# A Mamba block, cross attention and a gated dense layer on one core: the last chunk's dt, the scan's first loads and the first output projection arranged anew

## The chip, the cores and the metric

The kernel runs on one core of a Trainium2 chip. A core has five engines that run side by side, each working through its own instructions in order: TensorE (PE in the profile; PEld is its weight load), VectorE (DVE), ScalarE (ACT), GpSimd (POOL) and SyncE (SP), which here only issues transfers. ScalarE can issue transfers too; they go to a queue of their own (q10 in the profile, SyncE's is q1). The metric is the time of one execution on the device in microseconds (us), lower is better. The kernel before takes 3256.49 us, the median of three runs (3252.81 to 3258.94).

## The reference, cut to what matters

Four sequences of 1024 tokens with 512 features, all float32. The change touches only the first layer:

```python
h   = x + mamba(rmsnorm(x))            # this part
x   = layernorm(x + h + mlp(rmsnorm(h)))
x   = layernorm(x + cross_attention(x, ctx))
x   = layernorm(x + gated_lora_dense(x))

def mamba(x):                          # 1024 channels d, 16 states n
    u, z = split(x @ in_proj_w.T)
    u    = silu(causal_conv4(u))
    dt_r, B, C = split(u @ x_proj_w.T, [32, 48])
    dt   = softplus(dt_r @ dt_proj_w.T + dt_proj_b)
    h_l  = exp(dt_l * A) * h_(l-1) + dt_l * B_l * u_l      # scan over the tokens l
    y    = sum_n h * C + u * D
    return (y * silu(z)) @ out_proj_w.T
```

## The kernel before, in words

**Chunks.** The 4096 tokens are eight chunks (`NC`) of 512 (`T`). Every chunk goes through `mamba_in` first; then `scan_mlp` scans all chunks while TensorE does the output projection and the MLP of earlier chunks beside it; attention and the dense layer follow.

**`mamba_in`** works in *slots*, eight for each chunk (one for each block of 128 channels). Work that depends on earlier work is entered with `at(d, phase, f)`, for d slots later and one of four phases of a slot. `conv(j)` and `gate(j)` multiply by the input weights on TensorE; ScalarE and VectorE finish u and z; `x_proj` gathers u into one PSUM bank (`ps_xp`, pool `qp`); `project` copies it to `pr` and `bc` on ScalarE; `turn_c` transposes C and `put_c` stores it. For each block j, `dt(j)` is a matmul into one of two PSUM banks (pool `pd`), `dt_softplus` (ScalarE) makes r = dt from it, and for every second block `dt_u` stores r to memory, makes q = dt u on GpSimd (128x1024) and stores that. `put` stores through SyncE's queue. The table `AP` gives the distances: the dt matmuls are two to a slot from the second to the fifth slot after the last `x_proj`, the softplus a slot later, `dt_u` two slots after the matmul. For the last chunk these fall after the last input projection: slots (NC, 0) to (NC, 8) are run inside `mamba_in`, what is left after that (slot 9) in `rest()`, a generator that `scan_mlp` gets as `before`.

**`scan_mlp`** works in *quarters*, four for each step. A step k is one state n of one half chunk (four blocks of 128 channels, `GJ = 4`), 16 steps for a half chunk, 256 in all. In a quarter, VectorE scans one block (`scan`, `hs<-da,hs`), ScalarE makes the next factor (`exp`, `da`, two PSUM banks), GpSimd makes dt u B for half a step ahead in quarters 0 and 1 (`times_b`, `hs<-pk,b`), TensorE transposes the scanned blocks of the step before (`turn`, `ps_h`), and VectorE, or ScalarE with GpSimd, adds them times C to the sum `acc` (`times_c`). At the end of a half chunk `end` enters, some quarters later, the transposes back (`ps_y`), `add_u` (VectorE) and `times_z` (GpSimd), which leaves the finished y of a block; a transfer on ScalarE's queue stores it to memory. For the first two half chunks ScalarE's products wait in the large pool `b_z` (`hz`), which is closed before the MLP's pools (`b_w`, `b_x`, `b_g`: weights, x, hidden) take its room.

**The stream beside it.** From quarter 161 on (`until(GJ * 2 * NS + 33)`) the generator `stream` runs in each quarter after the transposes, paced by an estimate of TensorE's time. For each chunk: `Mlp(c)` loads x (`h`), `load_o` loads the four tiles of the output weights (`wo`, 512 KB each), `load_y` loads the stored y (`wy`, four tiles of 512 KB), `out_proj` multiplies (`ps_o`, 32 matmuls, two at most in a quarter), then a norm (`norm_h`, `norm_sq`, `norm_r`, `norm_x`), transposes (`turns`), and the MLP's products. `norm_r` is the reciprocal root on GpSimd: a scale and `rsqrt_p`, together 14 instructions on 128x4. For chunks 1 to 6, `run` starts the next chunk's projection at quarter 21 after the chunk's last scan. The last chunk is done after the scan.

**What sets the order.** Each engine's instructions are kept in the order of the program text within `mamba_in`, and within `scan_mlp` (`InOrder`), except SyncE's. Between the two functions, and on SyncE, the order is the compiler's, which places an instruction where its own time line says that it is ready. A new tile waits for the last use of the memory that it takes over.

Of the kernel before, what the change touches and what calls it, by code (L numbers as in the profile page):

```python
# [19 lines left out]
P = 128  # L20
# [4 lines left out]
NS = 16  # L25
# [124 lines left out]
EARLY_STEPS = 4  # L150
# [203 lines left out]
def mamba_in(tc, cn, a, dr, sx):  # L354
# [9 lines left out]
    with ExitStack() as ctx:  # L364
        up = sx.enter_context(open_pool(tc, "a_u", bufs=8, side="right"))
        pd = sx.enter_context(open_pool(tc, "a_pd", bufs=2, space=PSUM, side="right"))
        wp = ctx.enter_context(open_pool(tc, "a_w", bufs=1))
# [4 lines left out]
        qp = ctx.enter_context(open_pool(tc, "a_q", bufs=1, space=PSUM))  # L372
# [63 lines left out]
        class Step:  # L436
# [82 lines left out]
            def x_proj(self, j):  # L519
                if j == 0:  # L520
                    self.xp = qp.tile([P, T], F32, tag="xp", name="ps_xp")
                nc.tensor.matmul(
                    self.xp, wxp[:, j], self.u[j // 2][:, j % 2], start=j == 0, stop=j == KI - 1
                )
                if j == KI - 1:
                    at(1, 0, self.project)
                    at(1, 0, self.project_rest)
                    for b in range(KI):
                        at(*AP["b"][b], self.dt, b)
# [24 lines left out]
            def turn_c(self):  # L554

                ps = pp.tile([P, NT, P], F32, tag="mm", name="ps_c")
# [4 lines left out]
            def put_c(self, ps):  # L561
                ct = self.bc[:, 0 : NT * NS].rearrange("p (t n) -> p t n", n=NS)
# [8 lines left out]
            def dt(self, j):  # L571
# [6 lines left out]
                at(*AP["ds"], self.dt_softplus, j, ps, self.dts[jp][:, i])  # L578
                if i:
                    at(*AP["du"], self.dt_u, jp)  # L580
# [4 lines left out]
            def dt_u(self, jp):  # L585
# [3 lines left out]
                nc.gpsimd.tensor_tensor(q, r, self.u.pop(jp), ALU.mult)  # L589
# [55 lines left out]
        for n in range(9):  # L645
            slot(NC, n)

    def rest():
        n = 9
# [8 lines left out]
def scan_mlp(tc, cn, a, dr, before, bx, then):  # L658
# [8 lines left out]
    with ExitStack() as ctx, ExitStack() as sx:  # L667
# [11 lines left out]
        zps, tw = [], []  # L679

        class Step:
# [10 lines left out]
            def load(self, jp, q):  # L692

                pk = pks[self.g, jp, q] = kp.tile([P, 2, T], F32, tag=f"pk{q}", name=f"pk{q}")
                nc.sync.dma_start(pk, dr["pk"][self.c][2 * self.half + jp][:, :, q])
# [6 lines left out]
            def load_b(self):  # L702
                bs[self.k] = bp.tile([P, 1, T], F32, tag="b", name="b")
                nc.sync.dma_start(
# [128 lines left out]
            def times_z(self, i, y):  # L833
                nc.gpsimd.tensor_tensor(y[1], y[1], uzs.pop((self.g, i))[:, 1], ALU.mult)
                jp, jj = divmod(GJ * self.half + i, 2)
                at(1, 3, nc.scalar.dma_start, dr["y"][self.c][jp][:, jj], y[1])
# [11 lines left out]
        class Mlp:  # L848


            def __init__(self, c):
                self.c = c
                self.h = xp.tile([P, NT, D], F32, tag="h", name="h", bufs=2)
                nc.sync.dma_start(self.h, tokens(a["x"], c))
                self.ws, self.ps, self.gs, self.w3s = {}, {}, {}, []

            def w3_tile(self, name, late):
# [3 lines left out]
                return wp.tile([P, 2, D], F32R, tag="w3", name=name, bufs=4)  # L861

# [8 lines left out]
            def load_y(self):  # L871
                for jp in range(KI // 2):
# [10 lines left out]
            def out_proj(self):  # L883
# [7 lines left out]
                ys, ws = self.ys, self.wo  # L891
                for t in range(NT):
                    ps = pp.tile([P, D], F32, tag="mm", name="ps_o")
                    for j in range(KI):
                        jp, jj = divmod(j, 2)
                        nc.tensor.matmul(
                            ps, ys[jp][:, jj, t * P : (t + 1) * P], ws[jp][:, jj],
# [241 lines left out]
        for jp in range(2):  # L1139
            for i in range(2):  # L1140
                step(0).load(jp, i)
        step(0).load_c()
        for k in range(2):
            step(k).load_b()
        for jp in range(2):
            step(0).times_b(jp)
        for i in range(2):
            step(0).exp(i)
        for k in range(EARLY_STEPS):
            for q in range(GJ):  # L1150
                quarter(k, q, lambda: q % 2 or next(before, None))
        assert next(before, 0) == 0
        bx.close()
        with ExitStack() as zx:
# [4 lines left out]
            for k in range(EARLY_STEPS, 2 * NS + 8):  # L1159
# [31 lines left out]
        def first(mlp):  # L1191
            mlp.load_o()
# [10 lines left out]
        def last():  # L1203
            mlp = Mlp(NC - 1)
            yield from first(mlp)
# [4 lines left out]
        for k in range(2 * NS + 8, n + 2):  # L1210
# [855 lines left out]
```

## Time and profile before

| | us |
|---|---|
| median of three runs | 3256.49 |
| lowest, highest | 3252.81, 3258.94 |
| the profiled execution | 3250.26 |
| its span | 3248.5 |

| stretch of the span (us) | what runs there |
|---|---|
| 0 to 488 | `mamba_in` |
| 488 to 508 | dt of the last chunk, first loads of the scan |
| 508 to 2385 | the scan; from 741 on with output projections and the MLP |
| 2385 to 2700 | the last MLP work |
| 2700 to 3248 | attention and the dense layer |

Over the span TensorE is busy 92% of the time, VectorE 83%, GpSimd 73%, ScalarE 61%. The page's second part divides the span into 40 slices of 81 us and gives the busy tenths of each engine; the timeline gives instructions in order of time, several alike merged into one row (x4), with the idle time ahead of a row and what ended it in square brackets. The tiles' names tell the functions apart: nearly all instructions are issued through one helper and so have its line, L308.

### The profile page before, as it was taken

How to read it: one execution, taken by the hardware profiler on the slowest of the kernel's cores; microseconds unless marked ns; L12 is line 12 of the kernel's file. 1: busy time of each engine (PE TensorE's matmuls, PEld its weight loads, DVE VectorE, ACT ScalarE, POOL GpSimd, SP SyncE). 2: the span in 40 equal slices, each digit the busy share in tenths (PEclk: the TensorE clock that was granted, in tenths of full speed). 3: DMA queues.
4: the chain of work that ended last, by engine and by line, in shares of the span. 5: the costliest groups of instructions: out<-in, count | busy, mean ns of one | idle time of the engine just before them, and what ended most of it. 6: DMA issues, size and time to landing. Idle time of an engine off the chain costs nothing.

```text
span 3248.5 us, 47327 instructions
## 1 busy us (share of the span) xinstructions
PE 3001.8 (92%) x15992; PEld 2393.6 (74%) x15992; DVE 2698.2 (83%) x3836; ACT 1973.4 (61%) x3876; POOL 2369.2 (73%) x2169
## 2 busy tenths in 40 slices
PE   7999996887999999999999999999999997999987
PEld 5777773664876786786776786786785887898876
DVE  6876767997999999999999999999962346888876
ACT  3666666776666567666667666667642336666643
POOL 1334328998998999999999999999952115666664
PEclk9999995778999999999999999999999999999998
DMA  4778744336675775675765765765766432111110
GB/s 165 261 264 288 256 167 163 111 104 215 198 224 179 221 223 179 220 226 178 221 223 175 225 217 177 225 213 172 219 190 228 142 104 95 46 46 47 48 41 33
DMA packets 478472, 562.79 MB, mean 173 GB/s; under 512 B 46006, under 2 KB 309814, under 8 KB 477974
## 3 DMA queue, kind: packets, MB, share of 16 engines
q1 hardware_dynamic: 464406, 526.21, 50.6%
q10 hardware_dynamic: 13824, 33.56, 3.2%
q8 instruction: 127, 2.08, 0.3%
q14 instruction: 115, 0.94, 0.1%
HBM read 430.18 MB, written 129.50 MB: 172 GB/s over the span
## 4 chain that ended last, share of the span: by engine, by line
PE 34%; DVE 23%; POOL 12%; issue 8%; DMA 4%; ACT 3%; SPq 0%; ACTq 0%; DVEq 0%; POOLq 0%
DVE hs L308 10%; PE ps_ab L308 10%; POOL hs L308 6%; DVE acc L308 5%; PE ps_m L308 5%; PE ps_h L308 5%; PE ps_o L308 3%; PE ps_s L308 3%; PE ps_b L308 2%; POOL acc L308 2%; PE ps_y L308 2%; DVE g L308 1%; ACT da L308 1%; DMA uz<-pk 1%; DMA w<-w 1%
## 5 line engine op out<-in xcount | busy, mean ns | idle before, releaser
L308 DVE TENSOR_TENSOR_SCAN hs<-da,hs 128x512 f32<-128x512 f32 x1024 | 1214.7, 1207 | 42.7 <-ACT da L308 21.3
L308 POOL TENSOR_TENSOR hs<-pk,b 128x1024 f32<-128x1024 f32 x512 | 1217.2, 2393 | 29.7 <-issue 10.5
L308 ACT ACTIVATE da<-pk,aneg 128x512 f32<-128x512 f32 x1024 | 704.9, 689 | 554.3 <-DVE hs L308 548.6
L308 PE MATMUL ps_ab<-xn,w 128*128 128x512 f32 x3072 | 827.6, 406 | 0.0
L308 PE MATMUL ps_h<-ident,hs 128*128 128x128 f32 x4096 | 684.8, 292 | 91.0 <-DVE hs L308 47.3
L308 PEld LDWEIGHTS ps_h<-ident,hs 128*128 128x128 f32 x4096 | 535.5, 149 | 313.9 <-DVE hs L308 80.5
L308 PEld LDWEIGHTS ps_ab<-xn,w 128*128 128x128 f32 x3072 | 545.0, 189 | 95.8 <-issue 1.1
L308 PE MATMUL ps_m<-w,gs 128*128 128x512 f32 x1536 | 419.3, 408 | 9.5 <-POOL gs L308 9.5
L308 DVE SCALAR_TENSOR_TENSOR acc<-ps_h,c,acc 128x512 f32<-128x512 f32 x542 | 394.2, 727 | 37.8 <-PE ps_h L308 35.6
L308 POOL TENSOR_TENSOR acc<-acc,hc 128x512 f32<-128x512 f32 x232 | 300.1, 1293 | 52.9 <-ACT hc L308 51.5
L308 PEld LDWEIGHTS ps_m<-w,gs 128*128 128x128 f32 x1536 | 274.4, 191 | 61.7 <-POOL gs L308 14.5
L308 PE MATMUL ps_o<-wo,wy 128*128 128x512 f32 x512 | 247.8, 602 | 8.4 <-DMA wy<-y 5.1
L308 ACT ACTIVATE hc<-ps_h,c 128x512 f32<-128x512 f32 x344 | 231.3, 673 | 12.6 <-PE ps_h L308 12.5
L308 POOL TENSOR_TENSOR gs<-g,gs 128x512 fp32r<-128x512 f32 x128 | 165.8, 1295 | 85.1 <-ACT gs L308 85.1
L308 PE MATMUL ps_in<-xn,wu 128*128 128x512 f32 x768 | 214.7, 428 | 0.1
L308 POOL TENSOR_TENSOR pt<-pw,pt 128x512 fp32r<-128x512 f32 x48 | 62.7, 1306 | 194.9 <-ACT pt L308 131.2
L308 PE MATMUL ps_in<-xn,wz 128*128 128x512 f32 x768 | 191.8, 397 | 1.0 <-POOL wz L308 0.6
L308 PEld LDWEIGHTS ps_in<-xn,wu 128*128 128x128 f32 x768 | 145.3, 190 | 56.9 <-issue 22.0
L308 PEld LDWEIGHTS ps_in<-xn,wz 128*128 128x128 f32 x768 | 142.4, 188 | 34.8 <-POOL wz L308 1.1
L308 DVE SCALAR_TENSOR_TENSOR cv<-ps_in,pvec,cv 128x509 f32<-128x509 f32 (+2 forms) x192 | 143.3, 746 | 7.0 <-ACT cv L308 2.3
L308 ACT ACTIVATE hs<-hs,first 128x1 f32<-128x1 f32 x512 | 120.4, 284 | 27.1 <-POOL hs L308 11.7
L308 PEld LDWEIGHTS ps_o<-wo,wy 128*128 128x128 f32 x512 | 87.9, 194 | 66.5 <-issue 65.9
(244 smaller groups left out, 4623.9 us busy)
## 6 DMA issues: line engine op xcount, KB each, us to landing
w<-w SPq DMA_DIRECT2D x384, 512.0 KB, 5.6
b<-b SPq DMA_DIRECT2D x256, 256.0 KB, 4.1
pk<-pk SPq DMA_DIRECT2D x64, 512.0 KB, 6.7
w<-pt SPq DMA_DIRECT2D x48, 512.0 KB, 3.2
pk<-z SPq DMA_DIRECT2D x64, 256.0 KB, 2.9
pk<-u SPq DMA_DIRECT2D x32, 512.0 KB, 3.9
pk<-r SPq DMA_DIRECT2D x32, 512.0 KB, 3.1
pk<-q SPq DMA_DIRECT2D x32, 512.0 KB, 3.7
```

The source lines that it names most:

```text
L308: ins = f(*args, **kw)
```

## The change

In `mamba_in`, for the last chunk alone: the dt matmuls come two to a slot with their softplus in the same slot and `dt_u` right behind them, the product dt u goes to VectorE, and the transposed C takes one of the two dt banks. For every chunk the transposed C gets a tile of its own. Only slots (NC, 0) to (NC, 2) are run inside `mamba_in`; all that is left is in `rest()`. In `scan_mlp`, the first step's loads go to ScalarE's queue, b first, then dt u, then dt; the whole of `rest()` comes ahead of the first `exp`; the separate loop for the first four steps (`EARLY_STEPS`) is gone. The pool `b_z` is closed a step earlier. The first chunk's output weights, y and x are loaded from quarter 156 on, x last, and its projection starts at quarter 160 in place of 161. For chunks 0 to 6 the second half of y (blocks 4 to 7) stays in SBUF and is neither stored nor loaded. The first chunk's reciprocal root is made by VectorE (a scale and `rsqrt_v`, together 13 instructions).

In `mamba_in` (the last chunk is `self.c == NC - 1`):

```diff
-                        at(*AP["b"][b], self.dt, b)
+                        at(*(AP["b"][b] if self.c < NC - 1 else (2 + b // 2, 0)), self.dt, b)
...
-                ps = pp.tile([P, NT, P], F32, tag="mm", name="ps_c")
+                if self.c < NC - 1:
+                    ps = pp.tile([P, NT, P], F32, tag="mm", name="ps_c")
+                else:
+                    ps = pd.tile([P, NT, P], F32, tag="dt", name="ps_c")
...
-                ct = self.bc[:, 0 : NT * NS].rearrange("p (t n) -> p t n", n=NS)
+                ct = sp.tile([P, NT, NS], F32, tag="ct", name="ct", bufs=1)
...
-                at(*AP["ds"], self.dt_softplus, j, ps, self.dts[jp][:, i])
+                ds, du = (AP["ds"], AP["du"]) if self.c < NC - 1 else ((0, 1), (0, 2))
+                at(*ds, self.dt_softplus, j, ps, self.dts[jp][:, i])
                 if i:
-                    at(*AP["du"], self.dt_u, jp)
+                    at(*du, self.dt_u, jp)
...
-                nc.gpsimd.tensor_tensor(q, r, self.u.pop(jp), ALU.mult)
+                eng = nc.gpsimd if self.c < NC - 1 else nc.vector
+                eng.tensor_tensor(q, r, self.u.pop(jp), ALU.mult)
...
-        for n in range(9):
+        for n in range(3):
             slot(NC, n)
```

The y that is kept:

```diff
-                jp, jj = divmod(GJ * self.half + i, 2)
-                at(1, 3, nc.scalar.dma_start, dr["y"][self.c][jp][:, jj], y[1])
+                if self.half and self.c < NC - 1:
+                    kept.append(y[1])
+                else:
+                    jp, jj = divmod(GJ * self.half + i, 2)
+                    at(1, 3, nc.scalar.dma_start, dr["y"][self.c][jp][:, jj], y[1])
...
-                for jp in range(KI // 2):
+                for jp in range(KI // 2 if self.c == NC - 1 else KI // 4):
```

The root:

```diff
-                nc.gpsimd.tensor_scalar(
-                    self.ss, self.ss, 1.0 / D, 1e-5, ALU.mult, ALU.add
-                )
-                rsqrt_p(nc, sm, self.r, self.ss, "n")
+                eng, rsqrt = (nc.gpsimd, rsqrt_p) if self.c else (nc.vector, rsqrt_v)
+                eng.tensor_scalar(self.ss, self.ss, 1.0 / D, 1e-5, ALU.mult, ALU.add)
+                rsqrt(nc, sm, self.r, self.ss, "n")
```

The scan's start:

```diff
-        for jp in range(2):
-            for i in range(2):
-                step(0).load(jp, i)
+        step(0).load_b(nc.scalar)
+        for i in (1, 0):
+            for jp in range(2):
+                step(0).load(jp, i, nc.scalar)
+        step(1).load_b(nc.scalar)
         step(0).load_c()
-        for k in range(2):
-            step(k).load_b()
         for jp in range(2):
             step(0).times_b(jp)
+        for _ in before:
+            pass
         for i in range(2):
             step(0).exp(i)
-        for k in range(EARLY_STEPS):
-            for q in range(GJ):
-                quarter(k, q, lambda: q % 2 or next(before, None))
-        assert next(before, 0) == 0
         bx.close()
...
-            for k in range(EARLY_STEPS, 2 * NS + 8):
+            for k in range(2 * NS + 7):
```

The first output projection:

```diff
         def first(mlp):
-            mlp.load_o()
             yield from mlp.out_proj()
...
-            yield from until(GJ * 2 * NS + 33)
+            yield from until(GJ * 2 * NS + 28)
             mlp = Mlp(0)
+            mlp.load_o()
+            mlp.load_y()
+            mlp.load_h()
+            yield from until(GJ * 2 * NS + 32)
             yield from first(mlp)
...
-        for k in range(2 * NS + 8, n + 2):
+        for k in range(2 * NS + 7, n + 2):
```

More of the change, by code (lines that the diff above doesn't have):

```diff
@@ L149 @@
                 kind[g].add((n, t))
-EARLY_STEPS = 4
 H, DK, SK = 16, 32, 64
@@ L366, in mamba_in @@
         pd = sx.enter_context(open_pool(tc, "a_pd", bufs=2, space=PSUM, side="right"))
+        qp = sx.enter_context(open_pool(tc, "a_q", bufs=1, space=PSUM, side="right"))
         wp = ctx.enter_context(open_pool(tc, "a_w", bufs=1))
@@ L371, in mamba_in @@
         pw = ctx.enter_context(open_pool(tc, "a_pw", bufs=2))
-        qp = ctx.enter_context(open_pool(tc, "a_q", bufs=1, space=PSUM))
         pp = ctx.enter_context(open_pool(tc, "a_p", bufs=5, space=PSUM))
@@ L644, in mamba_in @@
         assert not later
-        for n in range(9):
+        for n in range(3):
             slot(NC, n)
     def rest():
-        n = 9
+        n = 3
         while slots.due:
@@ L678, in scan_mlp @@
         pks, bs, cts, accs, hcs, uzs, firsts = {}, {}, {}, {}, {}, {}, {}
-        zps, tw = [], []
+        zps, tw, kept = [], [], []
         class Step:
@@ L690, in __init__, with load @@
                 self.da = {}
-            def load(self, jp, q):
+            def load(self, jp, q, eng=nc.sync):
                 pk = pks[self.g, jp, q] = kp.tile([P, 2, T], F32, tag=f"pk{q}", name=f"pk{q}")
-                nc.sync.dma_start(pk, dr["pk"][self.c][2 * self.half + jp][:, :, q])
+                eng.dma_start(pk, dr["pk"][self.c][2 * self.half + jp][:, :, q])
             def load_c(self):
@@ L700, in load_c, with load_b @@
                     nc.sync.dma_start(cts[self.c], dr["c"][self.c])
-            def load_b(self):
+            def load_b(self, eng=nc.sync):
                 bs[self.k] = bp.tile([P, 1, T], F32, tag="b", name="b")
-                nc.sync.dma_start(
+                eng.dma_start(
                     bs[self.k], dr["b"][self.c][self.n : self.n + 1].partition_broadcast(P)
@@ L852, in __init__ @@
                 self.c = c
-                self.h = xp.tile([P, NT, D], F32, tag="h", name="h", bufs=2)
-                nc.sync.dma_start(self.h, tokens(a["x"], c))
+                if c:
+                    self.load_h()
                 self.ws, self.ps, self.gs, self.w3s = {}, {}, {}, []
@@ L861, in w3_tile, with load_h @@
                 return wp.tile([P, 2, D], F32R, tag="w3", name=name, bufs=4)
+            def load_h(self):
+                self.h = xp.tile([P, NT, D], F32, tag="h", name="h", bufs=2)
+                nc.sync.dma_start(self.h, tokens(a["x"], self.c))
             def load_o(self):
@@ L890, in out_proj @@
                     self.load_y()
-                ys, ws = self.ys, self.wo
+                ws = self.wo
+                ys = [y[:, jj] for y in self.ys for jj in range(2)]
+                while len(ys) < KI:
+                    ys.append(kept.pop(0))
                 for t in range(NT):
@@ L896, in out_proj @@
                         nc.tensor.matmul(
-                            ps, ys[jp][:, jj, t * P : (t + 1) * P], ws[jp][:, jj],
+                            ps, ys[j][:, t * P : (t + 1) * P], ws[jp][:, jj],
                             start=j == 0, stop=j == KI - 1,
@@ L1204, in last @@
             mlp = Mlp(NC - 1)
+            mlp.load_o()
             yield from first(mlp)
```

## The prediction, made before the changed kernel was built or run

> **What bounds the kernel now.** I read the page's busy shares first, then its 40 slices, then the timeline where VectorE's row has a hole. Shares alone would say TensorE (92%). The slices say otherwise:
>
> ```profile
> PE   7999996887999999999999999999999997999987
> ...
> DVE  6876767997999999999999999999962346888876
> ...
> POOL 1334328998998999999999999999952115666664
> PEclk9999995778999999999999999999999999999998
> ```
>
> A slice is 81 us. From the seventh slice (487 to 568 us) to the 29th VectorE stands at 7 to 9, almost always 9, while TensorE's granted clock sinks to 0.5 of full speed in places and the end isn't moved by that: through the scan VectorE sets the pace. In stretches of 20 us it is busy 1557 of 1660 us between 780 and 2440. So a microsecond in which VectorE stands still between 488 and 2385 us is, to first order, a microsecond of the result, and what other engines or transfers save there is worth nothing by itself. I therefore look for VectorE's holes that the change touches. There are three.
>
> Hole 1, VectorE's timeline at the scan's start (start, length, instruction, in brackets the idle time and what ended it):
>
> ```profile
> 489.17 0.68 DVE L308 TENSOR_TENSOR pr<-ps_xp,pr 32x512 fp32r<-32x512 f32 x1 [3.26 <-ACT bc L308]
> 508.08 4.64 DVE L308 TENSOR_TENSOR_SCAN hs<-da,hs 128x512 f32<-128x512 f32 x4 [18.23 <-POOL hs L308]
> 515.12 5.84 DVE L308 TENSOR_TENSOR_SCAN hs<-da,hs 128x512 f32<-128x512 f32 x5 [2.40 <-POOL hs L308]
> ```
>
> 18.23 + 2.40 us, both ended by GpSimd's dt u B. Why is GpSimd late? Its own timeline:
>
> ```profile
> 503.28 2.35 POOL L308 TENSOR_TENSOR q<-r,u 128x1024 f32<-128x1024 f32 x1 [2.72 <-issue]
> 505.57 0.19 POOL L308 COPY dt<-r 128x2 f32<-128x2 f32 x1
> 505.71 4.64 POOL L308 TENSOR_TENSOR hs<-pk,b 128x1024 f32<-128x1024 f32 x2
> 510.31 2.34 POOL L308 TENSOR_TENSOR q<-r,u 128x1024 f32<-128x1024 f32 x1
> ```
>
> The scan's product stands behind three of the last chunk's dt u, and each of those behind a softplus. ScalarE:
>
> ```profile
> 492.07 1.27 ACT L308 ACTIVATE r<-ps_dt,pvec 128x512 f32<-128x512 f32 x2
> 496.57 0.21 ACT L308 COPY bc<-ps_c 128x64 f32<-128x64 f32 x1 [3.24 <-DMA b<-bc]
> 496.68 1.27 ACT L308 ACTIVATE r<-ps_dt,pvec 128x512 f32<-128x512 f32 x2
> 497.97 1.28 ACT L308 ACT_TABLE_LOAD   x1
> 499.27 1.30 ACT L308 ACTIVATE da<-pk,aneg 128x512 f32<-128x512 f32 x2
> 500.58 1.28 ACT L308 ACT_TABLE_LOAD   x1
> 501.88 1.27 ACT L308 ACTIVATE r<-ps_dt,pvec 128x512 f32<-128x512 f32 x2
> ```
>
> Eight softplus, with 3.24 us lost on a copy that overwrites `bc` while its store still reads it, and two exps with two table changes put between.
>
> Holes 2 and 3, VectorE at the first output projection:
>
> ```profile
> 748.86 0.75 DVE L308 SCALAR_TENSOR_TENSOR acc<-ps_h,c,acc 128x512 f32<-128x512 f32 x1 [7.72 <-PE ps_h L308]
> ...
> 796.00 1.22 DVE L308 TENSOR_TENSOR_SCAN hs<-da,hs 128x512 f32<-128x512 f32 x1 [4.62 <-ACT da L308]
> ```
>
> In hole 2 the transposes stand behind the projection's first two matmuls, which start at 741.41 after 4.69 us of waiting for `wy` and take 3.75 us at half clock. In hole 3 GpSimd waits 2.79 us for the last square, works 787.44 to 791.29 on the root, then does 1.27 us of `norm_add`, and only then the scan's product.
>
> **Part 1, the last chunk's dt and the first loads.** The chain up to the table load that ends at 492.05 stays (last `x_proj` 488.04, casts to 489.14, subtraction to 489.85). From there: eight softplus at 0.635 us; but two banks serve them, so a matmul (0.69 us at half clock) must refill a bank, which makes about 0.75 us each, 6.0 us. The transposes of C in the same banks add one turn: 1.05 us (`ps_c` x4) + 0.21 us copy + a refill, about 1.5 us. Last softplus at 499.6, table load 1.28, first exp 0.65: 501.5. On VectorE dt u is two SBUF inputs, 128x1024: no row shows it. The nearest are `u<-u,cv`, 128x512, 0.66 us alone and up to 2.21, so 1.3 us is the floor; above, twice 1.1 us (the value at 484.85, beside a GpSimd product), 2.2, plus one GpSimd product of 2.35 to sit out: 4.6. I take 2.3 us for the last of the four (the other three lie in waits for softplus): done at 502.0. So the first scan starts at about 502.0, 6.1 us sooner. GpSimd, rid of 4 x 2.35 us, has both steps' products ready by then, so the 2.40 us also go: **8.5 us**, bounds 3 and 12.
>
> The Trainium skill speaks against this part: "SBUF — State Buffer", section "SBUF: two separate sides", says a VectorE instruction with two SBUF inputs and a GpSimd one that reads SBUF shut each other out for a whole instruction. The rows agree: `u<-u,cv` issued beside a GpSimd q (469.15 to 471.55) ends at 472.10, 0.55 us after it. By the rule each of the four dt u could lose 2.35 us; were all four exposed the part's gain would be gone.
>
> The loads: SyncE's queue moved 339 GB/s with its engines full from 488 to 503 us, so a load issued behind it comes late; on ScalarE's queue six issues cost some 0.35 to 0.45 us each (rows of `uz<-pk` there), 2.4 us, in the wait of 3.25 us for the last `x_proj`. If they were placed ahead of the last tanh (484.19) instead, the whole chain would be 2.4 us later; that is within my bounds. Of "DMA: Bandwidth & Descriptors", section "Issuing engines are not separate DMA queues", a second queue saves only issue time; if so, the loads land no sooner. No row here has both queues full; the sum needs b and dt u by about 497 only, ten microseconds after the issue.
>
> **Part 2, loads of the first projection.** SyncE issued `h` at 726.67 after waiting for the last back transposes (`ps_y`), whose tiles give up the room. That release stays, so the loads start no sooner though they stand five quarters earlier in the text. What changes is the order: before the first matmul came `h` (1 MB), four `wo`, one `b`, `wy`; now `h` comes last. At about 400 GB/s (406 in 735 to 741) 1 MB is 2.6 us, and a y store less 0.6: data at 738.1, not 741.4, 3.3 us sooner. But the projection's first matmuls also stand a quarter (1.9 us) sooner in TensorE's order, so the wait shrinks by less; walking the transposes through gives about 5 us of hole in place of 7.72. I take **3 us**, bounds 0 and 8 (all of hole 2, if the room is free sooner).
>
> **Part 3, the root on VectorE.** Thirteen small instructions at 0.16 to 0.17 us (VectorE's `rs_w` rows) are 2.1 us, from 787.44, when the squares are there; VectorE stood idle 0.76 us at that point, so its next two scans slip 1.2 us. GpSimd no longer waits and starts the scan's product some 6 us sooner, so of the 4.62 us all go; less 1.2: **3.4 us**, bounds 0 and 5.
>
> **Part 4, y kept in SBUF.** 7 x 4 stores and 7 x 2 loads, 14 MB of 562, go. In chunks 1 to 6 no hole hangs on them: at 1200 to 1240 us VectorE is busy 39.79 of 40. Work that hides them: the scan itself. I cost it at 0; SyncE's new order can help (VectorE waits 7.7 us in all for `uz`) or hurt: bounds +6 and -9 us over six chunks.
>
> **Sum.** 8.5 + 3 + 3.4 = 14.9, say 15 us. Profiled execution 3250.26 - 15 = 3235.3, span 3233.5; that execution lies 6.2 us below the median shown, so I forecast 3256.5 - 15 = **3241.5 us**. What remains late next: the scan itself, 1.2 us a block.
>
> **Rivals.**
> - *All of hole 2 goes, and the kept y helps.* Against: `h` waited for `ps_y`. For: SyncE itself was held 4.4 us just before by a `uz` that waited for GpSimd. 8.5 + 8 + 3.4 + 4 = 24 us: 3232.5.
> - *It doesn't do what it says.* The exps at 499.27 came ahead of softplus that the text puts first, so "in a row" may not hold; two exps and two table loads between (3.9 us), a dt u that sits out one GpSimd product (2.3), loads not sooner (part 2 at 0): 8.5 - 6.2 + 0 + 1 = about 3 us: 3253.5, no change.
> - *Slower: transfers in the six later chunks.* With two of the five `w12` tiles free and no y store to wait for, SyncE sends 512 KB weight loads earlier, into stretches whose DMA share is already 0.97 to 1.09 (1240 to 1260, 2220 to 2240); `uz` (6.8 us at 1309.31, VectorE waiting at its end) and `b` land later, and VectorE stands. At 2.5 us a chunk the gain is eaten; at 4.5 us, 27 - 15 = 12 us slower: 3268.5. Against: VectorE's present waits for transfers there are 7.7 us in all.
>
> **How the numbers follow.** A difference of 0.2% (6.5 us) is about what a measurement of this kernel can tell from none. Forecast (gain 8 to 20 us) 0.62, first rival 0.12, no change 0.12, slower 0.14. Faster 0.74, same 0.12, slower 0.14. The range reaches from 30 us of gain (the upper bounds of parts 1 to 3 with some of part 4) to 3.5 us of loss: 3226 to 3260.
>
> **What would show it.** Right: the eight softplus in one row without an exp between, the first scan at 500 to 504, no second wait of 2.4 us behind it; `ps_o` first at 8 to 14 us before 741 and VectorE's hole there 4 to 6 us; no `ss` row on GpSimd near 780 and a hole under 2 us; the distance of one chunk's projection to the next still 243 to 245 us. Wrong: a scan that waits for dt u on VectorE, ScalarE held at its loads before 488, or chunk distances that grow.

## The result, and the profile after

The changed kernel is **slower**: 3259.41 us, the median of 18 runs (3257.48 to 3265.10), against 3252.82 us (3249.6 to 3259.3, 18 runs) for the kernel before beside it (the three runs that the forecast started from gave 3256.49). The ratio is 1.0019, with a 95% interval of 1.0013 to 1.0025, so 6.6 us were lost where 15 were forecast as gained. The profiled execution took 3258.72 us, its span is 3256.9 us.

The 40 slices, the four rows that were shown of before:

```profile
PE   7999995887999999999999999999999998999987
...
DVE  6776767998999999999999999999962346888876
...
POOL 1334327997999999999999999999962115666664
PEclk9999995778999999999999999999999998999998
```

No digit moves by more than one, since a change of 0.2% is a tenth of a slice. What tells the kernels apart is the time between two numbered scans. VectorE's 1024 scans are counted from 0, so scan 128 is the one of quarter 128. The table has the differences of after to before, in us, cut at those scans; the start is the first instruction, 0.24 us into the span, and "last x_proj" is the end of the weight load of the last matmul into `ps_xp`. The matmul itself ends at 488.04 us of the span before and at 489.28 after (1.06 us long before, at a granted clock of 0.50, and 0.71 after, at 0.79); counted from there hole 1 grew by 3.9 us in place of 3.3.

| stretch | before | after | difference |
|---|---|---|---|
| start to last x_proj | 486.22 | 488.09 | +1.87 |
| last x_proj to scan 8 | 33.28 | 36.58 | +3.30 |
| scan 8 to 128 | 165.05 | 164.94 | -0.11 |
| 128 to 176 (hole 2) | 86.38 | 84.03 | -2.35 |
| 176 to 192 (hole 3) | 33.66 | 38.22 | +4.56 |
| 192 to 384 | 363.55 | 363.92 | +0.37 |
| 384 to 640 | 486.87 | 489.49 | +2.62 |
| 640 to 1023 | 733.11 | 732.97 | -0.14 |
| behind the last scan | 856.85 | 855.08 | -1.77 |

The first row is scatter: the sixteen profiles of whole kernels in this study reach that point between 486.2 and 491.5 us, with no order by their edits (before 486.2, loads_sync 486.3, both 488.6, in_a_row 491.5). The others I go through by the three holes.

**Hole 1** grew. VectorE's timeline at the scan's start:

```profile
499.28 0.68 DVE L307 TENSOR_TENSOR pr<-ps_xp,pr 32x512 fp32r<-32x512 f32 x1 [11.30 <-ACT bc L307]
...
508.96 2.34 DVE L307 TENSOR_TENSOR_SCAN hs<-da,hs 128x512 f32<-128x512 f32 x2 [2.57 <-ACT da L307]
...
514.15 2.34 DVE L307 TENSOR_TENSOR_SCAN hs<-da,hs 128x512 f32<-128x512 f32 x2 [1.43 <-ACT da L307]
...
520.30 5.83 DVE L307 TENSOR_TENSOR_SCAN hs<-da,hs 128x512 f32<-128x512 f32 x5 [2.38 <-POOL hs L307]
```

The subtraction into `pr`, which took place at 489.17, comes at 499.28. ScalarE's timeline tells why; the rows ACTq are its own DMA issues:

```profile
484.25 0.34 ACTq L307 DMA_DIRECT2D b<-b  x1
...
484.64 0.59 ACTq L307 DMA_DIRECT2D pk<-pk  x1
...
486.27 0.63 ACT L307 ACTIVATE u<-cv 128x512 f32<-128x512 f32 x1
492.16 5.10 ACTq L307 DMA_DIRECT2D pk<-pk  x3
497.29 0.85 ACTq L307 DMA_DIRECT2D b<-b  x1
498.19 0.58 ACT L307 CAST pr<-ps_xp 96x512 fp32r<-96x512 f32 x1 [11.29 <-DMA pk<-pk]
```

Two loads went out beside the last tanh. The third stands from 486.9 to 492.16 before it is issued, and behind it, in order, the cast that all eight softplus need. That cast comes 8.9 us behind its matmul, where before it came 0.03 us behind it. The softplus aren't in a row either:

```profile
506.88 1.28 ACT L307 ACT_TABLE_LOAD   x1
508.17 1.30 ACT L307 ACTIVATE da<-pk,aneg 128x512 f32<-128x512 f32 x2
509.49 1.28 ACT L307 ACT_TABLE_LOAD   x1
510.78 1.26 ACT L307 ACTIVATE r<-ps_dt,pvec 128x512 f32<-128x512 f32 x2
```

**Hole 2** shrank, to 3.77 + 1.24 us in place of 7.72:

```profile
747.05 0.75 DVE L307 SCALAR_TENSOR_TENSOR acc<-ps_h,c,acc 128x512 f32<-128x512 f32 x1 [3.77 <-PE ps_h L307]
...
751.28 0.75 DVE L307 SCALAR_TENSOR_TENSOR acc<-ps_h,c,acc 128x512 f32<-128x512 f32 x1 [1.24 <-PE ps_h L307]
```

**Hole 3** gave way to an instruction. VectorE, then GpSimd:

```profile
787.29 6.04 DVE L307 TENSOR_SCALAR ss<-ss 128x4 f32<-128x4 f32 x1 [1.20 <-ACT sq L307]
793.37 0.17 DVE L307 TENSOR_SCALAR rs_w<-ss 128x4 int32<-128x4 int32 x1
```

```profile
785.13 2.36 POOL L307 TENSOR_TENSOR hs<-pk,b 128x1024 f32<-128x1024 f32 x1
787.44 1.27 POOL L307 TENSOR_TENSOR h<-h,hn 128x512 f32<-128x512 f32 x1
788.66 4.64 POOL L307 TENSOR_TENSOR hs<-pk,b 128x1024 f32<-128x1024 f32 x2
802.01 1.27 POOL L307 TENSOR_TENSOR acc<-acc,hc 128x512 f32<-128x512 f32 x1 [8.71 <-ACT hc L307]
```

The root's first instruction, on four columns, is booked with 6.04 us. It ends 0.03 us behind GpSimd's last product (793.30); the next, just as small, take 0.17. I read the 6.04 us as time in which it was shut out.

### The profile page after: what moved, and what is told of

The parts are those of the page before. It is cut to its first block, busy times and chain, and to the rows that moved or that the text cites. A ratio compares the mean times of both kernels' runs of the same rounds, so it can differ in the third digit from the quotient of the medians.

```text
span 3256.9 us, 47232 instructions
## 1 busy us (share of the span) xinstructions
PE 2997.6 (92%) x15992; PEld 2392.3 (73%) x15992; DVE 2710.6 (83%) x3853; ACT 1972.7 (61%) x3878; POOL 2356.8 (72%) x2151
## 4 chain that ended last, share of the span: by engine, by line
PE 36%; DVE 24%; POOL 9%; issue 8%; ACT 3%; DMA 3%; SPq 0%; ACTq 0%; DVEq 0%; POOLq 0%
DVE hs L307 11%; PE ps_ab L307 10%; DVE acc L307 5%; POOL hs L307 5%; PE ps_h L307 5%; PE ps_o L307 5%; PE ps_m L307 5%; PE ps_s L307 3%; PE ps_b L307 3%; POOL acc L307 2%; PE ps_y L307 1%; DVE g L307 1%; ACT da L307 1%; DMA uz<-pk 1%; PE ps_num L307 1%
## 5 line engine op out<-in xcount | busy, mean ns | idle before, releaser
L307 PE MATMUL ps_o<-wo,wy 128*128 128x512 f32 x288 | 137.6, 609 | 3.8 <-DMA wo<-in_w_out_dram 2.4
L307 ACT ACTIVATE hs<-hs,first 128x1 f32<-128x1 f32 x512 | 120.5, 284 | 24.1 <-POOL hs L307 11.1
L307 POOL TENSOR_TENSOR q<-qf,q 128x256 fp32r<-128x256 f32 x64 | 47.6, 744 | 110.5 <-ACT q L307 108.7
```

Source lines behind the costliest of these rows:

```text
L307: ins = f(*args, **kw)
```

## The experiments

**What held ScalarE, read from the trace.** For each DMA issue the trace has the semaphore that it waits for and the one that its completion counts up. Eight completion semaphores are in use here, in turn, for both queues together. ScalarE's last four loads:

```
load (ScalarE's queue)  semaphore  earlier transfer with it, on SyncE's queue  its end   load issued
pk                      109        pk<-r, issued 484.98                        492.13    492.16
pk                      101        pk<-u, issued 488.00                        495.86    495.88
pk                      104        c<-c,  issued 488.61                        496.03    496.44
b                       107        (the first pk load)                         490.73    497.29
```

A load is issued only when the earlier transfer that bears its semaphore has ended. Two of the four were held by this, to 492.16 and to 495.88; the other two found their transfer ended and came as soon as the issues ahead of them were done. On SyncE such a wait holds only the transfers behind it. On ScalarE every instruction behind it stands too. The theory to test: this hold (a) and VectorE's shut-out root (b) make the loss; the rest of the change gains a few us.

**Undoing (a), (b) and both** (measured side by side; ratios to the kernel before).

```diff
 root_gpsimd
-                eng, rsqrt = (nc.gpsimd, rsqrt_p) if self.c else (nc.vector, rsqrt_v)
+                eng, rsqrt = nc.gpsimd, rsqrt_p
 loads_sync
-        step(0).load_b(nc.scalar)
+        step(0).load_b()
...
-                step(0).load(jp, i, nc.scalar)
-        step(1).load_b(nc.scalar)
+                step(0).load(jp, i)
+        step(1).load_b()
 in_a_row (both of the above, and)
-    pin = InOrder(tc, tc.nc)
+    pin = InOrder(tc, tc.nc, last)
```

> The changed kernel with one part undone: the first projection's root on GpSimd again, as in the kernel before. My theory: the root's first instruction on VectorE took 6.04 us because GpSimd's instructions beside it kept it out, so here the scan at 805 us after the start lies some 5 us sooner than in the changed kernel, VectorE has a hole of 4 to 5 us there again, and the time is about 4 us under that of the changed kernel, some 2 us over the kernel before. Rival (the loss lies in the six later chunks, through the kept y and SyncE's new order): the 5 us come back by the next chunk and the time stays within 1 us of the changed kernel's.

> The changed kernel with one part undone: the first step's six loads on SyncE's queue again. My theory: ScalarE stood 11.3 us at its own load issues, so here the cast of the last x_proj starts near 488 us as in the kernel before (498 in the changed one), and the scan's fourth instruction lies 6 to 10 us sooner; time 6 to 10 us under the changed kernel's, 0 to 3 under the kernel before. Rival (the exps between softplus, and dt u on VectorE, are the cost): the cast is sooner but the first scans gain under 3 us, and the time stays over the kernel before's. Second rival (the queue was right and the transfers are the limit): pk comes late on SyncE's queue as well, GpSimd waits for it until about 500, and the gain is under 3 us.

> The changed kernel with both undone: first step's loads on SyncE's queue and the first projection's root on GpSimd. What is left of the change is the dt in a row with dt u on VectorE, the first projection's loads ahead, and y half in SBUF. My theory: 6 to 10 us from the loads and 4 from the root add up, 10 to 14 us under the changed kernel, that is 4 to 8 under the kernel before. Rival (later chunks lose 2 us and more through the kept y): the scan's last instruction is 3 us or more later, against the scan at 805 us, than in the kernel before.

> The kernel named both, with one more edit: the written order of mamba_in's last instructions is kept against the scan's first ones, so that all eight softplus stand ahead of the first exps on ScalarE, as the text of the change has it. My theory: three of five table loads (1.28 us each) go, and the first scan lies 2 to 4 us sooner than in both, with no second wait of over 1 us behind it; time 2 to 4 us under both. Rival (the exps between softplus cost nothing, since the last dt u sets the second step's start): the first scan comes later by the 2 to 3 us that the softplus ahead of it take, the following ones without a wait, and the time is within 1 us of both.

| kernel | median us | ratio (95%) | x_proj to scan 8 | to scan 128 | 176 to 192 |
|---|---|---|---|---|---|
| before (beside these) | 3252.38 | 1 | 33.28 | 198.33 | 33.66 |
| root_gpsimd | 3253.65 | 1.0007 (0.9997 to 1.0016) | 36.70 | 201.64 | 30.24 |
| loads_sync | 3255.34 | 1.0008 (0.9999 to 1.0016) | 25.36 | 195.20 | 38.25 |
| both | 3246.79 | 0.9982 (0.9973 to 0.9991) | 25.37 | 195.88 | 30.25 |
| in_a_row | 3247.20 | 0.9980 (0.9972 to 0.9989) | 25.03 | 195.83 | 30.23 |

Each edit gains in its own stretch: the loads 11.2 us up to scan 8 (36.58 to 25.36), of which 4.9 are lost again by scan 128, the root 8.0 us at hole 3 (38.22 to 30.24). With both undone the kernel is 5.6 us under the kernel before. In the medians each edit alone is worth less than its stretch (3.9 us for the root and 3.6 for the loads by the ratios), both together 12.0; why they don't add up is not shown. The last edit did nothing, since with the loads on SyncE's queue the compiler had already put the eight softplus in one row; the exps between them came with the loads on ScalarE's queue. So the 11.2 us are not the hold alone: some 9 are the late cast, the rest came behind it, where those exps and their table loads stand. Against the kernel before, loads_sync is 7.9 us sooner at scan 8, but only 3.1 at scan 128. Where the other 4.8 go is seen at GpSimd in both:

```profile
522.17 4.64 POOL L307 TENSOR_TENSOR hs<-pk,b 128x1024 f32<-128x1024 f32 x2 [7.51 <-DMA b<-b]
```

and in SyncE's order in the same kernel, ahead of that b:

```profile
503.15 0.63 SPq L699 DMA_DIRECT2D pk<-pk  x1
...
504.72 0.62 SPq L699 DMA_DIRECT2D pk<-pk  x1
505.44 1.14 SPq L791 DMA_DIRECT2D uz<-pk  x1
...
508.96 0.56 SPq L791 DMA_DIRECT2D uz<-pk  x1
...
510.93 0.33 SPq L708 DMA_DIRECT2D b<-b  x1
```

Four loads of 512 KB that are needed some 90 us later (the next half chunk starts with scan 64, at 595.8 us), and stores of r and q between them, stand ahead of the fourth step's b, while the transfers run at some 400 GB/s (350 to 411 between 500 and 515 us). The b lands at 522.01, 11.1 us after its issue, and the issue itself came 0.06 us behind the end (510.87) of the first of the four loads, which bears the same semaphore.

**Two loads on ScalarE, b ahead, the root alone, y kept once.**

```diff
 root_vector_only (from the kernel before)
+                eng, rsqrt = (nc.gpsimd, rsqrt_p) if self.c else (nc.vector, rsqrt_v)
+                eng.tensor_scalar(self.ss, self.ss, 1.0 / D, 1e-5, ALU.mult, ALU.add)
+                rsqrt(nc, sm, self.r, self.ss, "n")
 kept_once (from both)
-                if self.half and self.c < NC - 1:
+                if self.half and self.c == 0:
 b_ahead (from both; called behind each load of pk and each load of uz on SyncE's queue)
+        def behind_b(load):
+            if last_b[0] is not None and now[0] < GJ * NS:
+                tc.add_manual_dep(load.ins, last_b[0].ins.name, ...)
 two_on_scalar (from in_a_row)
-        step(0).load_b()
+        step(0).load_b(nc.scalar)
+        step(0).load(0, 1, nc.scalar)
```

> The kernel before with one part of the change alone: the first projection's root on VectorE. My theory (VectorE's small SBUF-to-SBUF instruction waits until GpSimd's queue has a gap): an ss row of 3 to 7 us on VectorE near 790 us, the scan at 805 us no sooner or some 1 to 4 us later than in the kernel before, and the time 0 to 4 us longer. Rival (the loss of the changed kernel there came from the later start of that kernel's scan, not from the root): the ss row takes 0.2 us, the hole of 4.62 us goes and the scan at 805 us is some 3 us sooner.

> The kernel named both with y kept in SBUF for the first chunk alone: the six later ones store and load all of y, as in the kernel before. My theory: in both, the scan's last instruction comes 3.1 us later, against the scan at 805 us, than in the kernel before, and that drift is the price of the kept y and of the order of loads that goes with it; so here it goes, and the last scan lies 2 to 4 us sooner than in both, of which up to 2 us may be given back in the attention's tail; time 0 to 4 us under both. Rival (the drift is that of any kernel whose scan starts sooner, since later transfers set the pace): the drift stays at 3 us.

> The kernel named both, with one more edit: in the first 16 steps SyncE issues a load of pk or uz only behind the b loads that stand ahead of it in the text, so that the four loads of 512 KB that stood before the fourth step's b in SyncE's order come later. My theory: in both, that b landed 10.2 us after its issue, behind these 2 MB at 400 GB/s, and GpSimd and then VectorE waited for it (7.5 and 3.8 us); here GpSimd's wait falls under 3 us, VectorE's to under 1 us, and the scan's sixteenth instruction lies 3 to 4 us sooner against its fourth; time 2 to 4 us under both. Rival (the eight semaphores of the transfers or the stores ahead hold b as long): GpSimd's wait stays over 5 us and the time is that of both.

> The kernel named in_a_row with the first two of the six loads (b and one pk) on ScalarE's queue, the other four on SyncE's. In the changed kernel's trace each load on ScalarE's queue from the third on was issued within 0.05 us of the completion of a store of SyncE's queue that bears the same completion semaphore (eight of them are in use in turn); the first two found theirs free. My theory (the hold is the wait for that semaphore): with two loads ScalarE isn't held; the cast of the last x_proj starts as soon as its matmul ends, and the time is within 2 us of in_a_row. Rival (an issue on ScalarE's queue is slow whenever the transfer engines are full): ScalarE stands 3 us or more at its two issues, and the first scan comes 3 us or more later, against the last x_proj, than in in_a_row.

| kernel | median us | ratio (95%) | x_proj to scan 8 | to scan 128 | 176 to 192 | behind last scan |
|---|---|---|---|---|---|---|
| before (beside these) | 3254.71 | 1 | 33.28 | 198.33 | 33.66 | 856.85 |
| root_vector_only | 3256.84 | 1.0006 (0.9997 to 1.0014) | 33.55 | 198.60 | 36.23 | 855.14 |
| kept_once | 3252.90 | 0.9996 (0.9986 to 1.0006) | 24.62 | 195.03 | 30.24 | 863.98 |
| b_ahead | 3242.16 | 0.9960 (0.9948 to 0.9973) | 24.91 | 190.38 | 30.28 | 854.83 |
| two_on_scalar | 3246.26 | 0.9971 (0.9958 to 0.9983) | 24.47 | 192.59 | 30.27 | 859.26 |

*root_vector_only*: the root on VectorE is worth +2.6 us in the kernel before too. Its row, and GpSimd's beside it:

```profile
790.29 3.09 DVE L308 TENSOR_SCALAR ss<-ss 128x4 f32<-128x4 f32 x1 [1.98 <-ACT sq L308]
```

```profile
788.70 4.65 POOL L308 TENSOR_TENSOR hs<-pk,b 128x1024 f32<-128x1024 f32 x2
```

*b_ahead*: GpSimd's next two products start at 514.72 after 1.91 us for `ps_h`, no longer for b, and 7.95 of the 8.4 us gained at scan 8 are still there at scan 128. *two_on_scalar*: ScalarE isn't held at all:

```profile
483.76 0.35 ACTq L307 DMA_DIRECT2D b<-b  x1
...
484.15 0.59 ACTq L307 DMA_DIRECT2D pk<-pk  x1
...
489.65 0.58 ACT L307 CAST pr<-ps_xp 96x512 fp32r<-96x512 f32 x1 [3.25 <-PE ps_xp L307]
```

That agrees with the semaphores. It doesn't by itself exclude the rival, since the transfer engines weren't full at 484 us (62 GB/s in the changed kernel from 484 to 486); the two issues within 0.03 us of the end of the transfer with the same semaphore speak for the one and not for the other, and so do the four transfers that SyncE issued from 488.00 to 490.82 while ScalarE's third load stood. *kept_once* refuted my step on the drift: it stays (489.59 us from scan 384 to 640), and the kernel is some 4.5 us longer than both by the ratios, in its profile behind the last scan.

**Which part of the change gains, one by one.**

```diff
 kept_only: the kernel before with the change's y kept for chunks 0 to 6, nothing else
 dt_only: both, with these undone
-            yield from until(GJ * 2 * NS + 28)
+            yield from until(GJ * 2 * NS + 33)
-                if self.half and self.c < NC - 1:
-                    kept.append(y[1])
 proj_only: the kernel before with
-            yield from until(GJ * 2 * NS + 33)
+            yield from until(GJ * 2 * NS + 28)
+                if self.half and self.c == 0:
+                    kept.append(y[1])
 b_ahead_two: b_ahead with two_on_scalar's loads and in_a_row's order
 b_ahead_kept_once: b_ahead with kept_once's edit
```

> The kernel before with one part of the change alone: the second half of y of chunks 0 to 6 is kept in SBUF, not stored and loaded. My step (the kept y is worth nothing, since the scan covers those transfers): the distances of chunk to chunk are those of the kernel before within 1 us each, and the time is within 3 us of it. Rival (the kept y is what costs the 3 us between the scan at 1168 and that at 1655 us in every kernel with the change): the drift appears here and the time is 2 to 4 us longer. Second rival (kept_once was 4 us over both because the later chunks gain by the kept y): 3 to 5 us shorter, with the gain in the stretch behind the last scan.

> The kernel named b_ahead with the two edits of two_on_scalar: b and one pk of the first step on ScalarE's queue, and the written order kept between mamba_in's last instructions and the scan's first. My theory: the two loads find their completion semaphores free and GpSimd does its first product some 5 us sooner, so that the last dt u isn't held on VectorE by two products in a row (5.40 us for two of them in b_ahead); the first scan lies 0 to 2 us sooner against the last x_proj, and the time is that of b_ahead or up to 2 us less. Rival (the second pk now comes later and holds GpSimd's second product, as at 499 us in two_on_scalar): no sooner, or up to 2 us later.

> The kernel named b_ahead with y kept for the first chunk alone. If kept_once was 4 us over both because the kept y of the six later chunks is worth that much, this one is 3 to 6 us over b_ahead, most of it behind the last scan; if that was the scatter of the clock in the attention's part, it is within 2 us of b_ahead. The drift between the scans at 1168 and 1655 us (2 to 3 us against the kernel before) stays in both cases, since kept_once had it.

> The kernel named both without the first projection's new loads and without the kept y: of the change only the last chunk's dt in a row with dt u on VectorE is left, with the first loads on SyncE's queue. My reading of the runs so far: the scan's eighth instruction lies 5 to 8 us sooner than in the kernel before and its sixteenth 2 to 4 us (the rest is given back at the fourth step's b); hole 2 is back at 7 to 8 us; and if the drift of 2 to 3 us between the scans at 1168 and 1655 us belongs to the projection's phase, it is absent here. Rival (it belongs to the new start of the scan): it is here and absent in proj_only. Time 0 to 3 us under the kernel before.

> The kernel before with the first projection's part alone: its loads ahead with h last, all of it one quarter sooner, and y kept for the first chunk alone. If my step holds, hole 2 falls from 7.7 to about 5 us in all, and the scan at 771 us is 2 to 3 us sooner. If the drift of 2 to 3 us between the scans at 1168 and 1655 us belongs to the projection's phase (a quarter sooner in the written order), it is here, and the time is within 2 us of the kernel before; if it belongs to the scan's start, it is absent here and the gain of 2 to 3 us stays.

| kernel | median us (before) | ratio (95%) | to scan 128 | 128 to 192 | 192 to 640 | behind last scan |
|---|---|---|---|---|---|---|
| before (its profile) | | 1 | 198.33 | 120.04 | 850.42 | 856.85 |
| kept_only | 3248.81 (3254.59) | 0.9984 (0.9976 to 0.9993) | 198.44 | 119.39 | 850.45 | 850.05 |
| b_ahead_two | 3239.22 (3254.59) | 0.9956 (0.9943 to 0.9968) | 188.38 | 114.50 | 855.09 | 853.81 |
| b_ahead_kept_once | 3242.53 (3254.59) | 0.9965 (0.9952 to 0.9977) | 191.16 | 112.71 | 854.17 | 857.24 |
| dt_only | 3255.81 (3251.38) | 1.0010 (1.0002 to 1.0019) | 198.10 | 120.52 | 852.54 | 861.95 |
| proj_only | 3255.20 (3251.38) | 1.0011 (1.0002 to 1.0020) | 198.43 | 114.61 | 855.96 | 860.17 |

The projection's part gains 5.4 us between scan 128 and 192, 2.0 at hole 2 and 3.4 at hole 3, and gives 5.5 back by scan 640: alone it gains nothing. The dt part alone has nothing left at scan 128, and loses 2.1 on the way to scan 640. By their ratios both are slightly slower than the kernel before, by some 3 us. Both carry the drift, so neither of the two rivals about its owner holds; root_vector_only and kept_only don't have it. **What this drift is stays open.** The kept y is worth some 5 us by itself in kept_only (ratio 0.9984). The six chunks it was thought to matter in don't move (850.45 against 850.42). In the profiles the difference lies behind the last scan: 854.4 us there on the mean of the ten profiles with y kept in all chunks (850.1 to 859.3), 859.2 on that of the six without (855.1 to 864.0). But that doesn't show that the kept y shortens this stretch, for the clock granted to TensorE differs there too: 0.98 in kept_only (850.05 us, the fastest of its 11 runs), 0.97 in the kernel before (856.85), 0.96 in kept_once (863.98) and in dt_only (861.95). The clock may account for most of the difference between the ten and the six; no run here parts the two. Nor does the gain come again on top of b_ahead: against it, b_ahead_kept_once loses only 0.4 us by the medians and 1.6 by the ratios. **Where the kept y gains, and whether it always does, stays open.** b_ahead_two has the lowest median of the study, 14 us under the kernel before by the ratio and 15 by the medians; from b_ahead (0.9960) it can't be told apart.

**How long GpSimd keeps VectorE out.** Three benches, each run once, in which nothing of the block is computed, and one edit of the changed kernel (`root_other` writes the root's first result to a tile of its own).

```diff
 port
+                for i in range(beside):
+                    nc.gpsimd.tensor_tensor(big[3], big[0], big[1], ALU.mult)
+                nc.vector.tensor_scalar(ps[:, 0:4], mark, 0.5, None, ALU.mult)
+                for i in range(3):
+                    form()
 port_no_gap
-                    nc.gpsimd.tensor_tensor(big[3], big[0], big[1], ALU.mult)
+                    nc.gpsimd.tensor_tensor(big[2 + i], big[0], big[1], ALU.mult)
 port_forms (the form named as_in_kernel; the others leave out a line or write elsewhere)
+                for i in range(NT):
+                    nc.scalar.activation(sq, hn, AF.Square, accum_out=t[:, i : i + 1])
+            nc.vector.tensor_tensor_scan(va, ps, hn, 0.0, ALU.mult, ALU.add)
+            nc.vector.tensor_scalar(t, t, 1.0 / D, 1e-5, ALU.mult, ALU.add)
 root_other
-                eng.tensor_scalar(self.ss, self.ss, 1.0 / D, 1e-5, ALU.mult, ALU.add)
+                eng.tensor_scalar(ms, self.ss, 1.0 / D, 1e-5, ALU.mult, ALU.add)
```

> A bench in place of the whole computation (nothing of the block is computed): GpSimd works 6, 3 or 0 products of 128x1024 one behind the other, and VectorE, released as they begin, does three instructions of one form: a product of two sums of 128x4 from SBUF to SBUF (tensor_scalar), tensor_tensor 128x4, tensor_scalar from PSUM, scalar_tensor_tensor 128x512 with one input in PSUM, tensor_tensor 128x1024 (the form of dt u), tensor_scalar 128x512, and the scan with its decay in PSUM. My theory: the forms with all inputs and outputs in SBUF and no PSUM (tensor_scalar at least, tensor_tensor likely) wait until GpSimd's last product of the row, 10 us or more beside six and 4 us or more beside three, and take 0.2 us (128x4) alone; the forms with an input in PSUM aren't held. Rival (one product in progress is sat out, then the two engines take turns): the first instruction waits 2.4 us at most beside six as beside three.

> The bench named port with one edit: each of GpSimd's products writes a tile of its own, so that none waits for the one ahead of it (in port each did, and left a gap of 0.08 us, in which VectorE's instruction came through: no wait there was longer than 3.3 us). Nothing of the block is computed. My theory (VectorE's instruction waits until GpSimd leaves a gap, however short): the first small tensor_scalar beside six products waits until the row's end, 10 us or more, and beside three 5 us or more. Rival (it waits for the one product in progress, and the 6.04 us in the changed kernel had another cause): no wait over 2.4 us.

> A second bench in place of the whole computation (nothing of the block is computed): GpSimd works the row of the changed kernel without a pause (product with b read twice, the addition h<-h,hn in the second place's wake, four more products in all), and beside it VectorE does one tensor_scalar of 128x4, once in each of six ways: in place alone; in place behind a scan from PSUM; behind ScalarE's four squares that write its input, to another tile; the same in place; the same with a scan ahead; behind a ScalarE copy. In port_no_gap such an instruction waited for one product at most, in three kernels it waited 6.04, 6.08 and 3.09 us, over two to four GpSimd instructions, to the end of the row. If the way it is used there makes the difference, one of the six shows a wait of 4 us or more and the first doesn't; if none does, the wait over several instructions stays unexplained.

> The changed kernel with one edit: the root's first instruction on VectorE writes a tile of its own in place of overwriting the sum of squares. If writing in place makes VectorE wait over several of GpSimd's instructions, the row of this instruction falls from 6.04 us to 2.4 us at most; if not, it stays at 3 to 6 us and ends again within 0.05 us of the end of GpSimd's last product before a pause.

In port and in port_no_gap my theory fell: no instruction waited over more than one product, gap or not. VectorE's rows in port_no_gap, three small instructions beside three products, then alone, then three with a PSUM input beside six products:

```profile
23.80 6.80 DVE L307 TENSOR_SCALAR sout<-small 128x4 f32<-128x4 f32 x3
...
31.11 0.57 DVE L307 TENSOR_SCALAR sout<-small 128x4 f32<-128x4 f32 x3
...
54.65 0.55 DVE L307 TENSOR_SCALAR sout<-ps 128x4 f32<-128x4 f32 x3
```

Each of three takes a whole product, 2.27 us, where it takes 0.19 alone; with an input in PSUM it isn't held, nor are the scan and scalar_tensor_tensor from PSUM. In port_forms, the six ways of use in their order:

```profile
10.89 1.26 DVE L307 TENSOR_SCALAR ss<-ss 128x4 f32<-128x4 f32 x1
24.07 0.94 DVE L307 TENSOR_SCALAR ss<-ss 128x4 f32<-128x4 f32 x1
38.70 9.59 DVE L307 TENSOR_SCALAR so<-ss 128x4 f32<-128x4 f32 x1 [2.95 <-ACT sq L307]
51.84 1.48 DVE L307 TENSOR_SCALAR ss<-ss 128x4 f32<-128x4 f32 x1 [2.94 <-ACT sq L307]
64.71 1.48 DVE L307 TENSOR_SCALAR ss<-ss 128x4 f32<-128x4 f32 x1 [1.69 <-ACT sq L307]
74.79 14.81 DVE L307 TENSOR_SCALAR ss<-ss 128x4 f32<-128x4 f32 x1 [0.15 <-ACT ss L307]
```

Four came in at the first change from one GpSimd instruction to the next. Two did not, and stayed out over five and eight instructions, until GpSimd paused (the last one into the sums that close the bench, up to a pause of 0.08 us at 89.57). Neither writing in place, nor a scan ahead, nor ScalarE's squares divide the two from the four; in root_other the row still has 6.07 us. In the kernels it was out to the end of the row four times of four: 6.04, 6.08 in loads_sync, 3.09 in root_vector_only, 6.07, each time ending 0.03 us behind GpSimd's last product. So a wait can last one GpSimd instruction or a whole unbroken row of them; what decides between the two is open.

## Why the prediction was wrong

Two terms of the sum failed, each because an engine had to wait where I counted only its own work: the issues on ScalarE and the root on VectorE.

**Part 1 (forecast -8.5, bounds -3 to -12; measured +3.2 up to scan 128).** The step that failed is "six issues cost some 0.35 to 0.45 us each ... 2.4 us, in the wait of 3.25 us for the last `x_proj`". The price of an issue was nearly right (0.34 and 0.59 us for the two that went out freely). What it left out is that an issue can wait, and that ScalarE waits with it: 11.29 us ahead of the cast, where the forecast had the 3.25 us of before. I even asked for it in the last line ("ScalarE held at its loads before 488") without a price. The rest of the step was nearly exact: with the loads on SyncE's queue scan 8 came 7.9 us sooner and the first scan at 502.98 (forecast 502.0), with dt u on VectorE at 1.23 us where nothing held it and the eight softplus in a row. But "b and dt u by about 497" covered the first two steps only; the fourth step's b took 4.8 us back, a wait that the later start of the scan had hidden before.

The rule of the Trainium skill on the shared port that I set against this part ("SBUF — State Buffer", section "SBUF: two separate sides") held in one place: `q<-r,u` of two instructions took 5.41 us in loads_sync where two free ones take 2.46, beside two of GpSimd's products, 6.62 us where they take 4.64. Some 3 us were lost, not the 9.4 that four held dt u would have cost.

The other rule of the Trainium skill ("DMA: Bandwidth & Descriptors", section "Issuing engines are not separate DMA queues") says that a second queue saves only issue time. Here the first `pk` took 6.1 us from issue to landing on ScalarE's queue and 6.3 on SyncE's in loads_sync; it landed sooner (490.73 against 494.40) by as much as it was issued sooner. The held loads lost that again: the next `pk` landed at 500.33 against 496.53, and GpSimd's second product, after 7.17 us for it, ended at 502.7 against 501.9. No run has all six on ScalarE's queue without the hold.

**Part 2 (forecast -3).** Right in its place and nearly in size, 3.77 + 1.24 us of hole for "about 5". The first `ps_o` matmul came at 742.4, counted from scan 128 4 us sooner than before; the sign that I had set, 8 to 14 us before 741, didn't come and doesn't follow from the 3.3 us of the part itself. Not foreseen: 3.4 us more at hole 3 (176 to 192 in proj_only), and 5.5 us given back by scan 640.

**Part 3 (forecast -3.4; measured +4.6, and +8.0 against the same kernel with the root on GpSimd).** The step that failed is "Thirteen small instructions at 0.16 to 0.17 us (VectorE's `rs_w` rows) are 2.1 us". The twelve behind the first took 2.06 us up to the next scan (793.37 to 795.43). The first stood 6.04 us, and VectorE, which sets the pace, with it. I had weighed the port for dt u and not for this one, though its input and its output both lie in SBUF, and GpSimd's row beside it (`hs`, `h`, `hs`, `hs`) was in the profile.

**Part 4 (forecast 0).** Right for the six chunks. As a price for the whole kernel it was too low: about 5 us gained (kept_only), I can't say where.

**Sum.** By stretches: +1.9 scatter, +3.2 hole 1, -2.3 hole 2, +4.6 hole 3, +3.0 from scan 192 to 640, -0.1, -1.8 at the end: +8.4 between the two profiled executions, +6.6 between the medians. The rival that ended slower named another mechanism (transfers of the later chunks), so that its direction came true is luck. A gain of 15 us was there: b_ahead_two, in which ScalarE isn't held, the root is GpSimd's and the fourth b isn't late, has it. That it is the size of the forecast is luck too, for it is another sum: -9.9 up to scan 128, -5.5 to scan 192, +4.7 to scan 640, -3.0 behind the last scan.

## What to carry to other kernels

A load issued by a compute engine is an instruction of that engine: before moving one there, ask what its issue can wait for (here, for an older transfer with the same one of eight completion semaphores, on whatever queue) and what stands behind it. A tiny instruction that works from SBUF to SBUF on VectorE cost here what GpSimd was doing at that moment, up to a whole row of it, so leave it on the engine with the row (8.0 us here), or give it an input in PSUM, as in the benches. And when a start is pulled forward, follow the transfers of the next steps too, for what was hidden by the late start is late next.

## What the runs showed of the hardware that wasn't expected

A tensor_scalar of 128x4 from SBUF to SBUF took 0.16 us alone and up to 14.81 us beside GpSimd; the same from PSUM 0.16 us beside rows of GpSimd products. Two streams of 128x1024 products, VectorE's and GpSimd's, took turns at 3.25 us each in port (alone 1.24 and 2.34), so VectorE lost 2.0 us on each and GpSimd 0.9. Of six small instructions beside rows without pauses, four waited for the change to the next GpSimd instruction and two until GpSimd paused. And ScalarE stood 11.29 us with loads of its own queue ahead of it, two of which were issued within 0.03 us of the end of transfers of the other queue.
